# Accumulating DMAs for two block sums, and a third Strassen-Winograd step in one product

## The chip, the cores and the metric

The kernel runs on one core of a Trainium2 chip. A core has five engines with their own instruction queues: TensorE (PE in the profile) multiplies matrices into PSUM; VectorE (DVE), ScalarE (ACT) and GpSimd (POOL) work element by element; SyncE (SP) here only issues DMAs. ScalarE and GpSimd can issue DMAs too. An engine runs its queue in order and waits on semaphores for the others. The metric is the time of one execution on the device in microseconds, taken as the median of several runs.

## The reference

Two layers with residuals, on x of 8 sequences x 256 tokens x 1024 features, float32:

```python
# layer one: a dense layer plus a gated mixture of 8 rank-16 corrections
base   = einsum('btd,od->bto', x, W)
logits = einsum('btd,ed->bte', x, Wr) + 5.0 * one_hot(language_ids)[:, None, :]
topw, topi = top_k(logits, 2);  gates = the softmax of topw, put at topi
h      = einsum('btd,erd->bter', x, A)
x      = x + base + 2.0 * einsum('bter,bte,eor->bto', h, gates, B)
# layer two: each sequence has its own full 1024 x 1024 matrix of 16
x      = x + einsum('bsi,boi->bso', x, weight[adapter_ids])
```

The residual x is carried in the weights: the identity is added to W and to each adapter's matrix.

## The kernel before

**Layer one** is a product of a 1024 x 1024 matrix with 1024 x 2048 values, cut into 2 x 2 blocks: weights w11 to w22, inputs x11 to x22, results y11 to y22 (512 features by 1024 tokens each). The Strassen-Winograd scheme replaces the eight block products by seven, named "1" to "7" and run in the order 1, 5, 2, 6, 3, 7, 4. Their operands are sums of blocks, built in place by VectorE (`w_sum`, `x_sum`). Each block product is itself done by seven smaller products in the same way, in PSUM accumulators A, X and B. Function `product` writes one out by hand. Each smaller product is four matmuls in the source (two contraction chunks by two row tiles, 512 columns), which the profile counts as eight instructions, because it lists two per float32 matmul. The operands s1 to s3 and t1 to t3 are sums of quarters that `make_subs` plans for VectorE.

A y block has four quarters, `y[:, 0]` to `y[:, 3]`, each 128 partitions x 1024 elements (512 KB). A product adds its results to the quarters of `base` and writes them into those of `dest`. Where there is no base, `evict` is a copy on ScalarE; where there is one, it is an add on VectorE.

**The third step.** One of the seven smaller products multiplies two raw, unsummed quarters: X += a(0,1) b(1,0). With `deep` set, `third` does this one by seven still smaller products too, the pieces 1 to 7 (128 x 128 by 128 x 256, one contraction chunk). VectorE prepares six small operands ahead (r1, q1, r2, q2, r4, q4, planned no earlier than place 4 of the product before) and two more in between (`ops3`: r3, q3). Pieces 2, 3, 4 go into X. Pieces 1, 5, 6, 7 go into two single PSUM banks, and `take` adds them to the quarter `dest[:, 0]`. Products 5, 2 and 3 take this step; product 4 takes it twice; 6 and 7 (`make_subs(..., False)`) do not. Products 5, 2, 3 and 4 also accumulate low-rank matmuls (hg by b_sb or bdiff) into their accumulators; 6 and 7 have none.

The order inside a product with the third step is: A; piece 1; half of B; piece 5; A again, then VectorE's first add out of A (line 622, into quarter 1); piece 6; the other half of B and its add into quarter 3; pieces 2, 3, 4, 7 with their takes and the add of X into quarter 0; A a third time, then the second add out of A (line 644, into quarter 3); B and its add into quarter 1; A a last time (line 667) and its add into quarter 2.

**The filling work.** VectorE's other tasks stand in the list `todo` as (cost in us, earliest place, function). `pump(place)` is called at places 1 to 7 of every product. It takes the sum of all costs left, divides it by the places left (this one included), and issues tasks from the head of the list, leaving out those whose place has not come, until the rest of that share is 0.3 or less; at place 7 everything goes. Tasks are issued into the engine's queue where they stand, so this order is VectorE's order.

**The sums of whole y blocks.** `join(y12, y21)` and `join(y22, y21)` (lines 834 to 838) add y21 onto y12 and onto y22, a quarter per task, with the earliest places 4, 5, 6, 7 for quarters 0, 3, 1, 2. The first runs during product 3, which finishes y12 and leaves y21 alone; the second during product 7, which adds to y21. Product 7 and then product 4 rewrite y21. y12 and y22 hold the second half of the tokens, with which layer two starts.

**Layer two** runs per sequence (`adapt`), with one level of the same scheme. Its matrices are loaded by SyncE (`load_w1`, eight sets of four 1 MB blocks) into the room of x and w blocks of layer one that are no longer read; `prep_w1` and `prep_y` form the sums.

Of the kernel before, what the change touches and what calls it, by code (L numbers as in the profile page):

```python
# [12 lines left out]
ALU = mybir.AluOpType  # L13
# [12 lines left out]
def kernel(  # L26
# [26 lines left out]
    nc = tc.nc  # L53
# [56 lines left out]
    def yq(ij):  # L110

        return flat(yb[ij]).rearrange("p (q m n) -> p q m n", q=4, m=2)
# [103 lines left out]
    def tt(out_, x, y, op):  # L216
        nc.vector.tensor_tensor(out_, x, y, op)  # L217

    def add(out_, x, y):
        tt(out_, x, y, ALU.add)  # L220

    def minus(out_, x, y):
        tt(out_, x, y, ALU.subtract)
# [109 lines left out]
    todo = []  # L333
# [13 lines left out]
    def us(n):  # L347
        return (n + 151) / 960
# [9 lines left out]
    def x_sum(fn, out_, x, y):  # L358
        return pieces(fn, xb[out_], xb[x], xb[y], 4)
# [65 lines left out]
    def make_subs(key, w, x, further=True):  # L425

        def a(i, j):
            return wb[w][:, 2 * j : 2 * j + 2, i * OQ : (i + 1) * OQ]  # L430

        def b(i, j):
            return xb[x][:, 2 * i : 2 * i + 2, j * TQ : (j + 1) * TQ]

        t = {}

        def op(name, fn, x, y, first):
            pool = sub2 if name[1] == "2" else sub1
            width = OQ if name[0] == "s" else TQ

            def run():
                t[name] = pool.tile([P, 2, width], F32, name=f"{name}_{key}", tag=name)
                fn(t[name], *(t[v] if isinstance(v, str) else v for v in (x, y)))

            return us(2 * width), first, run

        def late_s():
            minus(t["s2"], a(0, 1), t["s2"])

        def late_t():  # L450
            minus(t["t2"], b(1, 0), t["t2"])

        deep = third(key, lambda: a(0, 1), lambda: b(1, 0)) if further else None
        subs[key] = (a, b, t, (late_s, late_t), deep)
        return [
            op("s1", add, a(1, 0), a(1, 1), 3),
            op("t1", minus, b(0, 1), b(0, 0), 3),
            op("s2", minus, "s1", a(0, 0), 3),
            op("t2", minus, b(1, 1), "t1", 3),
            op("s3", minus, a(0, 0), a(1, 0), 5),  # L460
            op("t3", minus, b(1, 1), b(0, 1), 5),
        ] + (deep[0] if further else [])
# [221 lines left out]
    def load_w1(u, *which):  # L684
        if u >= NB:
            return
        if u not in adapter:
            b = order[u]
            adapter[u] = nc.sync.value_load(aid_i[0:1, b : b + 1], min_val=0, max_val=NAD - 1)
        for ij in which:  # L690
            i, g = int(ij[0]) - 1, int(ij[1]) - 1
            nc.sync.dma_start(
                rawset[u % 2][ij], w1[bass.ds(adapter[u], 1), g, i].rearrange("a p k n -> p (a k) n")
            )
# [139 lines left out]
    y11, y12, y21, y22 = (yq(ij) for ij in IJ)  # L834

    def join(y, x):

        return [(1.22, p, lambda q=q: add(y[:, q], y[:, q], x[:, q])) for q, p in ((0, 4), (3, 5), (1, 6), (2, 7))]


    opening("1", y21)
# [45 lines left out]
    todo += t3[2:]  # L887
    product("6", y21, y21)
    load_w1(0, "21")
    todo += make_subs("7", "21", "11", False)  # L890
    t4 = x_sum(minus, "21", "21", "12")
    todo += t4[:2]
    todo += join(y12, y21)
    product("3", y22, y12, 2, 1)
    load_w1(0, "12", "22", "11")
    todo += t4[2:]
    todo += make_subs("4", "22", "21")
    todo += join(y22, y21)
    product("7", y21, y21)
    load_w1(1, "12", "11")  # L900
    todo += prep_w1(0, 0)
# [59 lines left out]
```

## Time and profile before

| | us |
|---|---|
| median of 3 runs | 427.61 (427.39 to 428.8) |
| profiled execution, its own time | 427.97 |
| its span, first to last instruction | 426.2 |
| TensorE busy | 421.2 (99%) |
| VectorE busy | 293.4 (69%) |
| ScalarE busy | 40.0 (9%) |
| GpSimd busy | 2.0 (0%) |
| product 3 on TensorE | from 145.6 to 176.1 |
| product 7 on TensorE | from 176.1 to 200.1 |
| product 4 on TensorE | from 200.1 to 230.2 |

The times of the products are read from TensorE's timeline. In those three stretches TensorE is busy throughout (30.5, 24.0 and 30.1 us), and VectorE for 23.6, 21.7 and 23.3 us. The DMA engines are busy 33%, 32% and 21% of them. A timeline line gives the start, the duration, the engine, the line of the kernel, the operation, what it writes and reads, the tile shapes and how many like instructions are merged; a bracket is idle time before it and what ended it. Line 217 is the helper that issues every VectorE sum, so such lines are told apart by their tiles: `y<-A,y` is an add out of accumulator A, `s` and `t` are operands of the next product, `r` and `q` those of the third step.

### The profile page before, as it was taken

What the parts mean: (1) busy time and instruction counts of PE and PEld (TensorE: products, weight loads), DVE (VectorE), ACT (ScalarE), POOL (GpSimd) and SP (SyncE); (2) the same over time, 40 slices, a digit from 0 to 9 for tenths busy, and PEclk for the clock granted to TensorE, in tenths of its full rate; (3) what the DMA queues carried; (4) which work ended last, traced back from release to release, by engine and by line L of the source; (5) the groups of instructions that cost most, each with busy time, mean ns of one, the idle gap of its engine ahead of it and who ended that gap; (6) DMA issues with size and microseconds to landing.
All of it is one profiled execution on the core that took longest, in us unless ns stands there. A gap on an engine that the chain in (4) does not pass through costs nothing.

```text
span 426.2 us, 3410 instructions
## 1 busy us (share of the span) xinstructions
PE 421.2 (99%) x1264; PEld 220.4 (52%) x1264; DVE 293.4 (69%) x409; ACT 40.0 (9%) x67; POOL 2.0 (0%) x10
## 2 busy tenths in 40 slices
PE   8999999999999999999999999999999999999996
PEld 6579975445444454444455444444444444444574
DVE  1646799857999859889598766665747666665531
ACT  2010122020000000000000101010110101010110
POOL 1000000000000000000000000000000000000000
PEclk9999999999999999999999999999999999999999
DMA  8995000000000230720202285565648385550202
GB/s 282 381 399 222 2 0 2 0 0 2 0 0 1 74 125 6 288 100 0 100 0 98 98 282 213 212 214 213 248 173 309 110 288 205 204 192 0 98 2 99
DMA packets 14305, 55.83 MB, mean 131 GB/s; under 512 B 1232, under 2 KB 3536, under 8 KB 9808
## 3 DMA queue, kind: packets, MB, share of 16 engines
q1 hardware_dynamic: 12976, 54.68, 35.7%
q10 hardware_dynamic: 1248, 0.93, 0.7%
q8 instruction: 10, 0.16, 0.2%
q14 instruction: 7, 0.06, 0.0%
q0 software_dynamic: 64, 0.00, 0.0%
HBM read 47.22 MB, written 8.39 MB: 130 GB/s over the span
## 4 chain that ended last, share of the span: by engine, by line
PE 95%; DVE 3%; issue 0%; POOL 0%; ACT 0%; POOLq 0%; DVEq 0%
PE A L741 23%; PE A L479 22%; PE B L741 13%; PE B L479 12%; PE ps_h L245 7%; PE X L741 6%; PE X L479 4%; PE A_last L799 3%; PE P L411 1%; DVE y L217 1%; DVE x L217 1%; PE X L411 1%; PE idle L495 1%; PE A L411 1%; DVE w L217 1%; PE P_1a L411 0%
## 5 line engine op out<-in xcount | busy, mean ns | idle before, releaser
L741 PE MATMUL B<-x,x 128*128 128x512 f32 x128 | 57.5, 592 | 0.0
L479 PE MATMUL A<-t,s 128*128 128x512 f32 x112 | 50.3, 592 | 0.0
L741 PEld LDWEIGHTS B<-x,x 128*128 128x128 f32 x128 | 24.3, 190 | 29.8 <-issue 29.7
L741 PE MATMUL A<-w,x 128*128 128x512 f32 x88 | 39.6, 592 | 0.0
L741 PE MATMUL A<-w,y 128*128 128x512 f32 x88 | 39.1, 592 | 0.0
L217 DVE TENSOR_TENSOR w<-w,w 128x1024 f32<-128x1024 f32 x24 | 28.9, 1221 | 14.0 <-PE A L741 14.0
L245 PEld LDWEIGHTS ps_h<-y,x 128*128 128x128 f32 x256 | 31.7, 190 | 3.3 <-issue 2.9
L479 PEld LDWEIGHTS A<-t,s 128*128 128x128 f32 x112 | 21.2, 190 | 22.9 <-issue 22.5
L245 PE MATMUL ps_h<-y,x 128*128 128x136 f32 x256 | 31.9, 279 | 0.0
L217 DVE TENSOR_TENSOR y<-A,y 128x1024 f32<-128x1024 f32 x19 | 23.2, 1221 | 11.5 <-PE A L479 11.3
L741 PEld LDWEIGHTS A<-w,x 128*128 128x128 f32 x88 | 16.7, 190 | 21.0 <-issue 21.0
L741 PEld LDWEIGHTS A<-w,y 128*128 128x128 f32 x88 | 16.7, 190 | 20.6 <-issue 20.6
L467 ACT COPY z<-A 128x512 f32<-128x512 f32 x21 | 12.3, 586 | 157.9 <-PE A L741 157.9
L479 PE MATMUL B<-t,s 128*128 128x512 f32 x56 | 25.9, 594 | 0.0
L479 PE MATMUL A<-x,w 128*128 128x512 f32 x56 | 25.3, 592 | 0.0
L479 PE MATMUL B<-x,s 128*128 128x512 f32 x48 | 21.6, 592 | 0.0
L217 DVE TENSOR_TENSOR x<-x,x 128x1024 f32<-128x1024 f32 (+1 forms) x20 | 19.3, 1002 | 0.0
L479 PE MATMUL A<-t,w 128*128 128x512 f32 x40 | 18.1, 595 | 0.1
L217 DVE TENSOR_TENSOR y<-B,y 128x1024 f32<-128x1024 f32 x12 | 14.6, 1219 | 5.1 <-PE B L479 5.1
L217 DVE TENSOR_TENSOR z<-X,z 128x512 f32<-128x512 f32 x8 | 5.5, 691 | 17.9 <-PE X L741 15.9
L217 DVE TENSOR_TENSOR t<-x 128x1024 f32<-128x1024 f32 x14 | 17.0, 1217 | 0.3 <-DMA x<-xT_dram 0.3
L217 DVE TENSOR_TENSOR t<-x,t 128x1024 f32<-128x1024 f32 x14 | 17.0, 1217 | 0.0
(166 smaller groups left out, 468.2 us busy)
## 6 DMA issues: line engine op xcount, KB each, us to landing
x<-w_dram SPq DMA_DIRECT2D x24, 1024.0 KB, 4.9
w<-w_dram SPq DMA_DIRECT2D x8, 1024.0 KB, 4.7
out_dram<-z SPq DMA_DIRECT2D x15, 512.0 KB, 3.0
x<-xT_dram SPq DMA_DIRECT2D x6, 1024.0 KB, 13.3
w<-wT_dram SPq DMA_DIRECT2D x3, 1024.0 KB, 15.5
x<-xT_dram SPq DMA_DIRECT2D x4, 256.0 KB, 3.9
x<-xT_dram SPq DMA_DIRECT2D x2, 512.0 KB, 6.8
w<-w11T_dram SPq DMA_DIRECT2D x1, 512.0 KB, 5.6
```

What stands on the lines that cost most here:

```text
L217: nc.vector.tensor_tensor(out_, x, y, op)
L245: nc.tensor.matmul(ps[v][:, u * EA : (u + 1) * EA], lhsT=xk(k, j, c)[:, ts(r, P)], rhs=aw_sb[:, k, :], start=(first and k == some[0] and u ...
L411: nc.tensor.matmul(out_, lhsT=l, rhs=r, start=(n in (1, 5)), stop=True, skip_group_check=True)
L467: nc.scalar.copy(dest, acc)
L479: nc.tensor.matmul(acc[:, m, :], lhsT=l, rhs=r, start=(first and i < len(ms)), stop=(i >= len(steps) - len(ms)), skip_group_check=True,)
L495: nc.tensor.matmul(idle[:, 0, :P], lhsT=ident, rhs=ident, start=True, stop=True)
L741: nc.tensor.matmul(accs[name], lhsT=lhs[:, k // 2, k % 2, :], rhs=rhs[:, k, :], start=(first and k == 0), stop=(k == KH - 1), skip_group_c ...
L799: nc.tensor.matmul(acc, lhsT=lhs[:, k // 2, k % 2, :], rhs=rhs[:, k, ts(v, m)], start=(first and k == 0), stop=(k == KH - 1), skip_group_c ...
```

## The change

The tasks of `join` become DMAs that GpSimd issues: each reads a quarter of y21 and adds it to the quarter of y12 or y22 where that lies, in SBUF. Their cost in `todo` becomes 0.0 and their places stay. They move ahead of the tasks of `make_subs` in the list. Product 7's `make_subs` no longer has `False`, so that product 7 takes the third step, and its six small operands r1 to q4 join the tasks that product 3 issues.

```diff
     def join(y, x):
 
-        return [(1.22, p, lambda q=q: add(y[:, q], y[:, q], x[:, q])) for q, p in ((0, 4), (3, 5), (1, 6), (2, 7))]
+        return [
+            (0.0, p, lambda q=q: nc.gpsimd.dma_start(y[:, q], x[:, q], accum_op=ALU.add))
+            for q, p in ((0, 4), (3, 5), (1, 6), (2, 7))
+        ]
...
     product("6", y21, y21)
     load_w1(0, "21")
-    todo += make_subs("7", "21", "11", False)
+    todo += join(y12, y21)
+    todo += make_subs("7", "21", "11")
     t4 = x_sum(minus, "21", "21", "12")
     todo += t4[:2]
-    todo += join(y12, y21)
     product("3", y22, y12, 2, 1)
     load_w1(0, "12", "22", "11")
     todo += t4[2:]
+    todo += join(y22, y21)
     todo += make_subs("4", "22", "21")
-    todo += join(y22, y21)
     product("7", y21, y21)
```

## The prediction

> **What bounds the kernel now.** I read the busy line, the chain, and then the timelines of TensorE and VectorE through layer one, the stage that the change touches.
>
> ```profile
> PE 421.2 (99%) x1264; PEld 220.4 (52%) x1264; DVE 293.4 (69%) x409; ACT 40.0 (9%) x67; POOL 2.0 (0%) x10
> PE 95%; DVE 3%; issue 0%; POOL 0%; ACT 0%; POOLq 0%; DVEq 0%
> ```
>
> TensorE is busy 99% of the span and its matmuls are 95% of the chain that ended last. Time is therefore gained only by removing TensorE work, and lost only by making TensorE wait. Product 7, in TensorE's timeline (start, duration, instruction):
>
> ```profile
> 176.06 3.60 PE L479 MATMUL A<-x,w 128*128 128x512 f32 x8
> 179.50 3.60 PE L479 MATMUL B<-t,s 128*128 128x512 f32 x8
> 182.93 3.60 PE L479 MATMUL A<-t,s 128*128 128x512 f32 x8
> 186.36 3.60 PE L479 MATMUL X<-x,w 128*128 128x512 f32 x8
> 189.80 3.60 PE L479 MATMUL A<-t,s 128*128 128x512 f32 x8
> 193.23 3.60 PE L479 MATMUL B<-x,s 128*128 128x512 f32 x8
> 196.66 3.60 PE L479 MATMUL A<-t,w 128*128 128x512 f32 x8
> ```
>
> Groups start every 3.433 us without a gap: four source-level matmuls are eight instructions of 0.429 us. A 128x256 piece (two instructions) paces at 0.43 us. Products 5, 2, 3 and 4 already take the third step. Product 2 shows what it can do (two lines of TensorE's timeline, one of VectorE's, one of the weight loads' waits in that stretch: total, times, longest):
>
> ```profile
> 114.33 1.88 PE L479 MATMUL B<-hg,bdiff 128*128 128x512 f32 x4
> 116.29 1.98 PE L479 MATMUL A<-t,w 128*128 128x512 f32 x4
> 115.02 1.22 DVE L217 TENSOR_TENSOR y<-A,y 128x1024 f32<-128x1024 f32 x1
> PEld A L479 <- DVE y L217: 0.9, 1, 0.9
> ```
>
> The last A group was due at 114.33 + 4 x 0.429 = 116.05. It started at 116.29, 0.05 after VectorE's add out of A ended (116.24). So this bank, read by VectorE between two uses, is the place where VectorE can hold TensorE. Product 3 runs the same order without x pieces in it (VectorE's timeline):
>
> ```profile
> 156.15 1.22 DVE L217 TENSOR_TENSOR y<-A,y 128x1024 f32<-128x1024 f32 x1 [2.88 <-PE A L479]
> 157.29 0.41 DVE L217 TENSOR_TENSOR y<-P,y 128x256 f32<-128x256 f32 x1
> 157.62 0.68 DVE L217 TENSOR_TENSOR s<-w,s 128x512 f32<-128x512 f32 x1
> 159.09 1.23 DVE L217 TENSOR_TENSOR y<-B,y 128x1024 f32<-128x1024 f32 x1 [0.78 <-PE B L479]
> 160.23 1.22 DVE L217 TENSOR_TENSOR t<-x,t 128x1024 f32<-128x1024 f32 x1
> 161.36 0.69 DVE L217 TENSOR_TENSOR s<-w 128x512 f32<-128x512 f32 x1
> 161.96 1.22 DVE L217 TENSOR_TENSOR t<-x 128x1024 f32<-128x1024 f32 x1
> 163.10 1.41 DVE L217 TENSOR_TENSOR y<-P,y 128x512 f32<-128x512 f32 x2
> 164.54 1.22 DVE L217 TENSOR_TENSOR y<-X,y 128x1024 f32<-128x1024 f32 x1
> 165.69 0.68 DVE L217 TENSOR_TENSOR s<-s,w 128x512 f32<-128x512 f32 x1
> 166.28 1.22 DVE L217 TENSOR_TENSOR t<-x,t 128x1024 f32<-128x1024 f32 x1
> 167.42 1.22 DVE L217 TENSOR_TENSOR y<-A,y 128x1024 f32<-128x1024 f32 x1
> ```
>
> From the first add out of A to the second: 11.27 us. With the bubble before B closed up (159.09 becomes 157.62 + 0.60 = 158.22, so 0.87 less) it is 10.40 us of back-to-back work. Product 3's low-rank matmuls give that stretch time. Product 7 has none.
>
> **What the skill says.** The Trainium skill's "DMA: Bandwidth & Descriptors", section "Anatomy of one DMA — SWDGE (gpsimd) path", prices a GpSimd DMA at about 2.0 us plus bytes / 436 GB/s: 3.2 us (estimate) for 512 KB. The trace's nearest rows agree in size: 512 KB stores land after 3.0 us, 1 MB loads after 4.7 to 4.9, GpSimd's two tiny DMAs after 4.4 to 4.6. "Collectives: The Full Stack", "The bandwidth ceiling", says an adding transfer reads two sources and costs double the reading, not the add: 1.2 us more (estimate); no row here shows an accumulating DMA. "SBUF — State Buffer", "Who interferes with whom", infers that a VectorE tensor_tensor does not block descriptor generation; untested here. "TensorE: Matmul & The Clock Gate", section on HAM oscillation, puts the idle gap that lowers the clock at about 3.4 us; the trace has no such gap after the opening.
>
> **The change, part by part.**
>
> 1. *Product 7's third step, TensorE.* Removed: the X group, four matmuls, 3.43 us. Added: seven pieces, 7 x 0.43 = 3.00. Gain 0.43 us, directly on the bound.
>
> 2. *Joins leave VectorE.* Eight adds at a pitch of 1.135 us, 9.1 us less of VectorE work. TensorE waits for none of them in products 3, 7, 4 (its only waits there are its own issue, 0.2 us each), so this alone is worth 0.
>
> 3. *Third step, VectorE.* In product 3, six small subtractions: 3 x 0.20 + 3 x 0.34 = 1.6 us, at places 6 and 7, in time the joins (4.5 us) leave. Free; without that room they would delay piece 5 of product 7, 5.5 us after product 3's end. In product 7: the 1.13 us X add stays, added are takes 1, 6 (0.34 each), 7, 5 (1.44 together) and r3, q3 (0.54): 2.7 us.
>
> 4. *Where pump puts work in product 7.* The list is now 2.44 (two x21 quarters) + 5.74 + 2.14 = 10.33 us, the joins count 0. Place 1: share 10.33/7 = 1.475; one quarter leaves 0.255, under 0.3, stop. Place 2: 9.11/6 = 1.518; the second quarter. Place 3: s1, t1. Place 4: join q0, s2, t2. So the second quarter falls into the stretch between the two reads of A.
>
> 5. *The stretch.* Product 7 starts at 176.06 as before. The A group that feeds the first add ends after A, p1, half B, p5, A = 2 x 3.433 + 0.43 + 1.717 + 0.43 = 9.44 us: 185.50. VectorE starts 0.27 later (as 156.15 against 155.88 in product 3): 185.77. It then has 10.40 + 1.13 (second quarter) = 11.53 us, every input of which is by then ready. The second add runs 197.30 to 198.52, and A can be written from 198.57. TensorE wants it after p6, half B, p2 to p4, p7, A, B: 185.50 + 0.43 + 1.72 + 1.29 + 0.43 + 3.43 + 3.43 = 196.23. Stall 2.34 us. This is unhidden: product 4 and layer two keep TensorE full to the end, so the delay is handed on. In product 4 VectorE is no later relative to TensorE (it drains at 204.1, before the first piece ends at 205.87).
>
> 6. *The DMAs and their waits.* POOL is otherwise empty after 2.7 us, so nothing queues behind these but one another; SP's loads keep their order. Each transfer must read y21 before the next product rewrites that quarter, a new wait on VectorE, behind which its whole queue stands. y12's issue at 165.8 (q0), 168.7, 172.7 (q1), 177.6; rewrites at 180.1, 189.0, 185.8, after 200. Least room: q1, 13.1 us. For y22: q0 issues at 195.6, is wanted at 205.9 (VectorE has 3 us of idling behind it); q1 10.5 us plus about 2 of slack. Low end of a transfer: 3.0. High: 4.5 + 2.4 (double data), doubled again for sharing with two 1 MB weight loads, 12. I take 5. Up to 12 all are hidden by the room; past 13 each us is a us. Four more DMA waits on VectorE: at most 0.05 each (the semaphore step seen above), 0.1 in the stretch; I take 0, since they are satisfied early. A gain from this part is excluded: nothing waited for the joins.
>
> 7. *Weight loads.* The load for x12's second half waits for the second x21 quarter, 7 us later than now (about 188.9 + pitch); landing near 194 to 200, it is first used past 240. Free.
>
> Sum: -0.43 + 2.34 = +1.91 us. The profiled execution took 427.97 (span 426.2, 1.8 around it), so 429.88; the median of the runs, 427.61, becomes 429.5.
>
> **Rivals.**
>
> *VectorE keeps up (ends not slower).* The stall vanishes or shrinks below the measurement if the second x21 quarter runs before the first add out of A, where VectorE idles 2.9 us. Place: pump's place 1. Price: 1.13 us; then stall 1.21, net +0.78, 428.4. It decides at a share of 0.3; the sum gives 0.255, so it needs an error of mine in the list. The same mechanism with the stretch 0.64 us shorter than I count also ends within measurement. Speaking for the bare gain (427.2): VectorE's total in product 7, about 20 us of 23.6, fits on average. Against: product 2's measured stall, with more TensorE time to spare.
>
> *Accumulating DMAs are slow.* If a transfer's data takes d, q0, q3 and q1 follow one another: 3 + 3d must fit 20 us before VectorE's first add in product 7, and about 18.4 in product 4 with its slack. It decides at d = 5.1 to 5.7 us. At d = 6: 1.0 + 2.6 on top, 433; at 8: about 445. For: the row is missing, and loads share the engines (share 0.41 to 0.51 from 165 to 190). Against: 1 MB lands in 4.9.
>
> *The clock drops.* A stall of 2.3 us is under the skill's 3.4; if it counted, a window at half speed adds some 1.7: 431.2.
>
> That the joins stay on VectorE can't be: the instruction is gone from its queue.
>
> **How the numbers follow.** Forecast 0.70, 429.0 to 430.3 (stall 1.8 to 3.1). VectorE keeps up 0.13: 0.12 within, 0.01 faster. Slow DMAs 0.14. Clock 0.03. A measurement of this kernel tells about 0.3% (1.28 us) from no change: bounds 426.33 and 428.89. Slower: 0.70 + 0.14 + 0.03 = 0.87. The range 428.4 to 433 leaves out the bare gain (0.07) and the worst DMA cases (0.09).
>
> **What would show it.** TensorE should show one gap of about 2.3 us before product 7's last A group, released by VectorE's add into y21, and no other new one; product 7 without it 23.6 us. VectorE should run without idling from 185.8 to 198.5, with an x21 piece after the s subtraction. The DMAs should land about 5 us after issue, with no VectorE wait on a DMA. The prediction fails if that gap is under 1.7 us, if a DMA wait appears ahead of an add into y21, or if product 4 stalls as well.

## The result, and the profile after

The change made the kernel slower: 430.82 us median of 4 runs (430.63 to 431.87) against 427.81 (the three runs of the kernel before and one more), a ratio of 1.0072 with a 95% interval of 1.0048 to 1.0096. Run again later, five runs gave 431.11 against 427.90, and 1.0072 (1.0059 to 1.0086). The prediction said 429.5, range 428.4 to 433.0.

The busy line and the chain (engines' shares of the work that ended last) of the kernel after:

```profile
PE 421.5 (98%) x1270; PEld 221.6 (52%) x1270; DVE 288.6 (67%) x413; ACT 40.1 (9%) x67; POOL 9.0 (2%) x18
PE 92%; DVE 6%; issue 0%; POOL 0%; ACT 0%; DVEq 0%; POOLq 0%
```

TensorE's share of the chain fell from 95% to 92% and VectorE's doubled, although VectorE does 4.8 us less in all (288.6 against 293.4). It is one place. TensorE's timeline at the end of product 7:

```profile
193.27 3.60 PE L479 MATMUL B<-x,s 128*128 128x512 f32 x8
199.02 3.70 PE L479 MATMUL A<-t,w 128*128 128x512 f32 x8 [2.15 <-DVE y L217]
202.56 3.60 PE L479 MATMUL A<-x,w 128*128 128x512 f32 x8
```

The last A group was due at 193.27 + 3.43 = 196.70 and started 2.32 us late, released by VectorE's add into y21. (The bracket, 2.15, counts from the modelled end of the matmul before, 3.60 after its start; both measures name the same gap.) Three lines of VectorE's timeline, the first add out of A, the x21 quarter, and the second add:

```profile
186.22 1.22 DVE L217 TENSOR_TENSOR y<-A,y 128x1024 f32<-128x1024 f32 x1 [2.86 <-PE A L479]
188.29 1.22 DVE L217 TENSOR_TENSOR x<-x,x 128x1024 f32<-128x1024 f32 x1
197.75 1.22 DVE L217 TENSOR_TENSOR y<-A,y 128x1024 f32<-128x1024 f32 x1
```

197.75 - 186.22 = 11.53 us; VectorE does not idle between them. TensorE has no other new gap.

To compare kernels apart from the opening, I read off TensorE's timeline when product 3 starts and how long it is from there to the first matmul of layer two. That stage holds all that was changed; from its end to the issue of the last output every one of the 13 profiles takes 192.94 or 192.95 us. The gap is counted from the due start, and each ratio is against runs of the kernel before taken beside it:

| kernel | product 3 starts | stage | gap before the last A | median, ratio (95%) |
|---|---|---|---|---|
| before | 145.58 | 84.59 | none | 427.81 to 427.96 |
| the change | 146.03 | 86.60 | 2.32 | 430.82, 1.0072 (1.0048, 1.0096) |
| joins only | 144.95 | 84.60 | none | 428.10, 1.0009 (1.0001, 1.0017) |
| step only | 146.35 | 86.58 | 2.29 | 430.85, 1.0067 (1.0054, 1.0080) |
| quarter first | 146.42 | 85.50 | 1.2 | 429.33, 1.0029 (1.0022, 1.0037) |
| late operands | 145.09 | 84.19 | none | 427.96, 1.0003 (0.9994, 1.0011) |
| late, joins on VectorE | 145.38 | 84.74 | none (0.46 in product 4) | 428.35, 1.0008 (0.9998, 1.0018) |
| twice the traffic | 146.59 | 94.72 | 1.0 (and 6.5 in the third step) | 438.66, 1.0246 (1.0231, 1.0262) |
| two more adds | 145.02 | 91.66 | 4.6 | 434.67, 1.0164 (1.0150, 1.0178) |

The stage grew by 2.01 us where the prediction had 1.91. The rest of the difference between these two profiled executions, 0.45 + 0.14 us, is a later start of product 3 and a longer end. But the medians of the runs grew by 3.0. The experiments were made to tell whether the gap is the third step's or the joins', and where the last us comes from.

### The profile page after: what moved, and what is told of

Read it like the earlier page. It is cut to its first block, busy times and chain, and to the rows that moved or that the text cites. A ratio compares the mean times of both kernels' runs of the same rounds, so it can differ in the third digit from the quotient of the medians.

```text
span 428.8 us, 3453 instructions
## 1 busy us (share of the span) xinstructions
PE 421.5 (98%) x1270; PEld 221.6 (52%) x1270; DVE 288.6 (67%) x413; ACT 40.1 (9%) x67; POOL 9.0 (2%) x18
## 3 DMA queue, kind: packets, MB, share of 16 engines
q1 hardware_dynamic: 12976, 54.68, 35.6%
## 4 chain that ended last, share of the span: by engine, by line
PE 92%; DVE 6%; issue 0%; POOL 0%; ACT 0%; DVEq 0%; POOLq 0%
PE A L741 22%; PE A L479 21%; PE B L741 13%; PE B L479 11%; PE ps_h L245 7%; PE X L741 6%; PE A_last L799 3%; PE X L479 3%; DVE y L217 3%; PE P L411 2%; DVE x L217 1%; DVE t L217 1%; PE X L411 1%; PE idle L495 1%; PE A L411 1%; DVE s L217 1%
## 5 line engine op out<-in xcount | busy, mean ns | idle before, releaser
L217 DVE TENSOR_TENSOR y<-A,y 128x1024 f32<-128x1024 f32 x19 | 23.2, 1220 | 16.3 <-PE A L479 13.3
L217 DVE TENSOR_TENSOR y<-P,y 128x512 f32<-128x512 f32 (+1 forms) x17 | 9.5, 561 | 11.1 <-PE P L411 10.4
```

## The experiments

**Each half alone.** First the accumulating joins without the third step (a diff against the kernel after):

```diff
-    todo += make_subs("7", "21", "11")
+    todo += make_subs("7", "21", "11", False)
```

> The joins as accumulating DMAs ahead of the operands, product 7 without the third step. If VectorE's stretch in product 7 is the whole cause: no gap on TensorE there, product 7 back at 24.0 us, time that of the kernel before (427.8, within 0.5). If the DMAs themselves cost (their traffic, their waits on VectorE, or the instructions that GpSimd gains), up to the 3.0 us of the change: a gap released by a DMA, or about 1 us spread over product 3, 7 or the opening, 428.8 to 430.8.

TensorE's timeline of the group that had the gap:

```profile
196.04 3.60 PE L479 MATMUL A<-t,w 128*128 128x512 f32 x8
```

The stage took 84.60 us, the same as before to 0.01; no gap, no wait on a DMA. The ratio of the runs is 1.0009, about 0.4 us, and their medians differ by 0.14. Some 0.2 us of it stands at the very end: from the issue of the last output to the end of the span it is 425.8 - 422.50 = 3.3 us, in every profile with GpSimd's transfers 3.2 to 3.3, without them 3.0 to 3.1.

Then the third step alone (a diff against the kernel before, whose joins stay as they are):

```diff
-    todo += make_subs("7", "21", "11", False)
+    todo += make_subs("7", "21", "11")
```

> The third step in product 7 alone; the joins stay VectorE adds where they stood. VectorE's stretch then loses the second x21 quarter (the fuller list puts both at place 1) and gains s2 (no change) and r1, q1, r2, q2 in place of it: 10.40 + 1.08 = 11.48 us, so a gap of about 2.3 us in the same place and 2.0 us more than before in product 7: 429.8. If the DMAs are what costs, no gap and about 427.4; if the DMAs were needed to make room for the step, clearly worse than the change, over 432.

TensorE's timeline in this kernel:

```profile
199.31 3.70 PE L479 MATMUL A<-t,w 128*128 128x512 f32 x8 [2.12 <-DVE y L217]
```

It is the same gap, 2.29 us, and the same stage (86.58). The stretch here runs from 186.54 to 198.04, 11.50 us: the x21 quarter is out of it, and r1, q1, r2, q2 are in. So the loss belongs to the third step, with product 4's operands where they stand. Moving the joins neither caused it nor prevented it, although it took 9 us of work off VectorE. The runs were 2.9 us slower, again more than the stage's 2.0.

**What stands in the stretch.** Two edits of the kernel after move VectorE's tasks out of it and take no work away:

```diff
-    todo += t4[2:]
+    todo += [(0.9, p, f) for us, p, f in t4[2:]]
```

> The change, with the planned cost of the last two x21 quarters set to 0.9 so that both fall at place 1, where VectorE idles. By the stretch theory it is 1.13 us shorter (10.40), the gap 1.2 us, the time 1.1 us under the change: 429.7. If DMAs or something outside product 7 set the loss, no difference: 430.8.

```diff
-    todo += make_subs("4", "22", "21")
+    todo += [(us, max(p, 5), f) for us, p, f in make_subs("4", "22", "21")]
```

> The change, with every operand of product 4 planned no earlier than place 5 of product 7. The stretch loses s1, t1, s2, t2 (3.47 us): 8.06 us, and VectorE's add out of A ends about 195.5 where TensorE wants A at 196.7 (times of the change's profile): no gap, product 7 takes 23.6 us, 2.4 us under the change and 0.4 under the kernel before: 428.4 against 430.8, or 427.4 against 427.8. If the DMAs cost about 1 us apart from the gap, it stays at 428.5 to 429.

With a planned cost of 0.9 both x21 quarters fall at place 1, into VectorE's idle time. VectorE's timeline there, and TensorE's at the gap:

```profile
181.31 2.35 DVE L217 TENSOR_TENSOR x<-x,x 128x1024 f32<-128x1024 f32 x2
198.30 3.70 PE L479 MATMUL A<-t,w 128*128 128x512 f32 x8 [1.05 <-DVE y L217]
```

The gap shrank by 1.1 us, the length of one quarter's subtraction, and the stage with it (86.60 to 85.50). With the operands of product 4 late, VectorE's second add out of A follows the add out of X directly, and TensorE runs through:

```profile
192.20 1.23 DVE L217 TENSOR_TENSOR y<-X,y 128x1024 f32<-128x1024 f32 x1
193.34 1.22 DVE L217 TENSOR_TENSOR y<-A,y 128x1024 f32<-128x1024 f32 x1
195.77 3.60 PE L479 MATMUL A<-t,w 128*128 128x512 f32 x8
```

VectorE finishes the second add at 194.56, 1.2 us before TensorE wants A. Product 7 takes 199.20 - 175.58 = 23.62 us and the stage 84.19, 0.40 less than in the kernel before: the whole 0.43 us of the saved piece, less rounding. The time of the runs does not show it (1.0003, 0.9994 to 1.0011). With the 0.2 us at the end set against it, about 0.2 would be left (an estimate), less than these runs can tell.

**Whether the joins have to be DMAs for that.** The late order with VectorE's joins, against the kernel before:

```diff
-    todo += make_subs("7", "21", "11", False)
+    todo += make_subs("7", "21", "11")
...
-    todo += make_subs("4", "22", "21")
+    todo += [(us, max(p, 5), f) for us, p, f in make_subs("4", "22", "21")]
```

> No accumulating DMAs: the joins as VectorE adds where the kernel before has them, product 7 with the third step, and product 4's operands not before place 5 of product 7. If moving the joins to DMAs is what makes room for the step, TensorE waits here in product 7 or at the start of 4 by 1 us or more. If only the order inside the stretch counts: product 7 in 23.6 us, at most a gap of 0.3 us before product 4's B, and a time within 0.3 us of the late-operand version with DMAs (428.0).

Product 7 takes 23.62 us here too. Product 4's first B then starts 0.46 us after it was due, held by VectorE (TensorE's timeline):

```profile
203.81 1.98 PE L479 MATMUL B<-t,s 128*128 128x512 f32 x4 [0.29 <-DVE y L217]
```

So the stage is 84.74. This is the only place found where the DMAs of the joins are worth something: 84.74 - 84.19 = 0.55 us, once the order is mended. The medians, 428.35 and 427.96, can't confirm so little: their ratios' intervals overlap.

**How much room the transfers had.** This kernel adds each quarter of y21 onto y11 as well while product 3 runs, so that the DMA engines carry twice as many joins there:

```diff
-            (0.0, p, lambda q=q: nc.gpsimd.dma_start(y[:, q], x[:, q], accum_op=ALU.add))
+            (0.0, p, lambda q=q, d=d: nc.gpsimd.dma_start(d[:, q], x[:, q], accum_op=ALU.add))
             for q, p in ((0, 4), (3, 5), (1, 6), (2, 7))
+            for d in ((y, y11) if y is y12 else (y,))
```

> The change, with every quarter of y21 that the first join adds onto y12 also added onto y11 by a second accumulating DMA (so the rows of the first half of the tokens come out wrong; only the traffic counts). In the change's profile the eight DMAs took 5.4% of 16 engines' span, 2.9 us of all engines each, and quarter 1's landed 10.9 us after its issue at 173.3, at 184.2, 2.0 us before VectorE rewrites it at 186.2. Three more DMAs ahead of it or beside it are 8.7 us: it lands near 193, VectorE's first add out of A starts then, and the delay is handed on in full: about 6.5 us over the change, 437.5. If the DMAs had ample room, as the prediction had it (up to 12 us hidden, 5 taken), the time stays at 430.8.

In the kernel after, the page has these lines on the queues (packets, MB, share of 16 engines; q0 carries the joins, q1 the loads and stores) and on the joins' issues (count, KB, median us to landing):

```profile
q1 hardware_dynamic: 12976, 54.68, 35.6%
q0 software_dynamic: 1216, 4.20, 5.4%
y<-y POOLq DMA_DIRECT2D x8, 512.0 KB, 6.6
```

In the span of 428.8 us, 5.4% is 23.2 us of all engines, 2.9 for each join. The loads and stores on q1 moved 54.68 MB in 35.6%, which is 1.46 us per 512 KB. So a join costs the DMA engines twice what a plain transfer of its size between SBUF and the chip's main memory does; no plain transfer from SBUF to SBUF was run. One by one, y12's quarters landed 4.8, 9.6, 10.9 and 10.8 us after issue, with 1 MB weight loads issued between them, and y22's after 4.5, 4.7, 5.1 and 8.1. The third of y12, quarter 1, was issued at 173.3 and landed at 184.2; VectorE rewrites that quarter of y21 at 186.2. With twice the traffic, VectorE's and TensorE's timelines:

```profile
194.90 1.23 DVE L217 TENSOR_TENSOR y<-A,y 128x1024 f32<-128x1024 f32 x1 [10.97 <-DMA y<-y]
196.51 1.22 PE L411 MATMUL P<-q,r 128*128 128x256 f32 x2 [6.37 <-DVE y L217]
```

VectorE waited for the DMA until 194.9, where it was due at 186.8, and handed the delay on. The expected landing (near 193) was right within 2 us, and the time came out 1.2 us above 437.5, with the granted clock at 0.50 from 196 to 200 us, after this gap. The transfers of the change were hidden, but by no more than 2.0 us.

**The last us.** Two things vary from run to run. The opening: product 3 began anywhere from 144.95 to 146.59 in these profiles, with the same instructions before it; the first group of four matmuls took from 1.98 to 3.62 us, where four take 1.88 later on. These are the two ends, from TensorE's timelines of joins only and of twice the traffic:

```profile
4.24 1.98 PE L479 MATMUL X<-x,w 128*128 128x512 f32 x4
4.24 3.62 PE L479 MATMUL X<-x,w 128*128 128x512 f32 x4
```

And the mean clock: of the nine timed runs of the change (four, and the five of the repetition below), six had 1.0 (430.09 to 431.11 us) and three 0.994 to 0.996 (431.35 to 431.87); none of 55 runs of the kernel before was under 0.998. (What they lack to 1.0 costs nothing: in the profile of the kernel before the granted clock is under 1.00 only from 420 us on, 0.94 on average, where TensorE has all but finished.) The step alone, with the same gap and no joins as DMAs, has two of its five runs at 0.994 and 0.996 too. So the change was run again, and the gap made longer with two more adds in the stretch.

> The change itself, for its time over more runs and a second profile. Product 3 to the first matmul of layer two took 86.60 us against 84.59, 2.0 more, but the runs 3.0 more. If the opening's start of the clock is what varies (product 3 began at 145.0 to 146.4 in six profiles), the median comes down to 430.0 to 430.4 and the stage is again 86.6. If a clock that drops after the gap adds to it in a part of the runs, the median stays near 430.8 and some runs show a mean clock of 0.996 or less and 1 us more.

```diff
+    todo += [(0.0, 2, lambda q=q: add(y11[:, q], y11[:, q], y11[:, q])) for q in (0, 1)]
     todo += t4[2:]
```

> The change with two more VectorE adds of 1024 elements in the stretch (y11 onto itself, so the first half of the tokens comes out wrong). By the stretch theory the gap grows by 2.27 us to 4.6 and the time by 2.3 us to 433.1. If a gap of this length lowers TensorE's clock, the matmuls after it run at half speed for some time: a mean clock of 0.995 or less and 1 to 2 us more, 434 to 435.

The change again had a stage of 86.61 us. The two adds made a gap of 4.6 us, as expected, but cost 5.06 us in the stage over the change, not 2.27. TensorE's timeline there, and the stage's busy times (us; busy us and instructions of TensorE, weight loads, VectorE, ScalarE, GpSimd; granted clock; DMA share; GB/s):

```profile
200.28 6.48 PE L479 MATMUL A<-t,w 128*128 128x512 f32 x8 [4.42 <-DVE y L217]
200.00:203.00 3.00, 2.72 (x3) 1.18 (x4) 3.00 (x4) 0.00 (x0) 0.86 (x1) 0.50 1.01 190
```

The clock read half just after the gap, and the group took 6.48 us instead of 3.70: 2.27 + 2.78 = 5.05 us. All five timed runs had a mean clock of 0.990 to 0.996. Three more profiles of the change were taken to find the same in it.

> The change once more, for its profile alone. In nine timed runs the span was 428.3 to 429.3 at a mean clock of 1.0 (six runs) and 429.6 to 430.1 at 0.994 to 0.996 (three). If the gap of 2.2 us lowers the clock in those runs in which the opening was early, a profile at 0.996 or less shows product 3 starting before 145.6 and the last A group of product 7 longer than 3.7 us by 1 to 3 us; a profile at 1.0 shows it starting at 145.9 or later and the group at 3.7. If the low clock comes from elsewhere, the two are not tied.

> As the first look: early opening with a low clock after the gap, or late opening with a full one.

> As the first look: early opening with a low clock after the gap, or late opening with a full one.

TensorE's last A group of product 7 and the granted clock after it (the third number from the end of a window's line), in the first of the three:

```profile
198.03 5.40 PE L479 MATMUL A<-t,w 128*128 128x512 f32 x8 [2.16 <-DVE y L217]
198.00:200.00 2.00, 1.97 (x4) 0.93 (x5) 2.00 (x3) 0.00 (x0) 0.86 (x1) 0.73 1.06 197
200.00:202.00 2.00, 2.00 (x4) 0.91 (x3) 1.58 (x4) 0.00 (x0) 0.86 (x1) 0.50 1.03 197
202.00:204.00 2.00, 2.00 (x5) 0.76 (x4) 0.53 (x1) 0.00 (x0) 0.00 (x1) 0.91 0.93 174
```

and in the second:

```profile
198.82 3.70 PE L479 MATMUL A<-t,w 128*128 128x512 f32 x8 [2.16 <-DVE y L217]
200.00:202.00 2.00, 2.00 (x6) 0.83 (x5) 2.00 (x4) 0.00 (x0) 0.07 (x1) 1.00 0.99 184
```

The same gap of 2.16 us (by the bracket), once with the clock at half after it and once without. Granted 0.73, 0.50 and 0.91 in three windows of 2 us make up for some 3.4 us at half (an estimate). It costs 5.40 - 3.70 = 1.70 us, and the stage is 88.30 us instead of 86.61. The third profile is like the first (5.40 us, 88.30). Product 3 began at 145.04 and 145.51 in the two with the half clock, and at 145.82, 146.03 and 146.38 in the three profiles of the change without.

So, in these five, the executions that gain time in the opening lose more of it after the gap. No run of the change gets both right: the fastest of its nine has a span of 428.3 us, where the kernel before reaches 425.4, which is 2.9 less and not 2.0. An estimate shows that this is enough for the last us. The start of product 3 in a run of the kernel before can be worked out from its span, less 84.59, 192.95 and 3.08 us for what follows. Give each of the 55 runs 2.01 us for the stage, 0.15 for the end, and 1.70 more if its product 3 began by 145.51: the median rises by 3.1 us, and 26 of the 55 have the half clock. The two measurements were 3.0 and 3.2 us, and five of twelve executions. With the line drawn just under 145.82, the earliest start seen with a full clock in a profile, it would be 3.5 us. The half clock lifts the early half of the runs above the late half, and the median falls among late runs with a full clock.

Why the opening and the clock after the gap go together stays open: no run here set the one to see the other, and the granted clock reads 1.00 through the opening, in slow ones (3.62 us for the first four matmuls) as in fast ones (1.98).

## Why the prediction was right, point by point

- *What bounds, and the place.* Right. TensorE was held at the one place named, the last A group of product 7.
- *Steps 1, 4 and 5, the third step and the stretch.* Right in mechanism and size: seven pieces save 0.43 us (23.62 us for product 7 where nothing holds it), the quarter fell at place 2 as worked out from the shares, the stretch was 11.53 us as predicted, the stall 2.32 against 2.34. The stage's sum was +2.01 against +1.91; the 0.10 is in the first A group after the gap, 3.70 us instead of 3.60 even at full clock.
- *Step 2, the joins leave VectorE.* Right that this alone is worth nothing: 84.60 against 84.59.
- *Step 3.* Right. No piece of product 7 waited for its small operands.
- *Step 6, the DMAs.* Right that they are hidden, wrong on the margin. The 5 us I took is what most of y22's transfers took (4.5 to 5.1). In product 3, with one another and the weight loads, they took up to 10.9, and 2.0 us were left of a room of 12.9 (13.1 in the sum). The bound of 12 held, but it does not come out of its terms: 4.5 + 2.4, doubled, is 13.8. "Collectives: The Full Stack" in the Trainium skill, "The bandwidth ceiling", has an adding transfer cost double the reading. This trace agrees in size, 2.9 us of the engines against 1.46, though it does not show the reads one by one. The end of the kernel, 0.2 us later with GpSimd's transfers, was not in the sum.
- *Step 7.* Right. No weight load arrived late.
- *The rivals.* "VectorE keeps up" did not occur; the quarter put first shows what it would have been: stage +0.91 where it had +0.78. "DMAs are slow" did not occur, but twice the traffic showed its price. "The clock drops" is where the point went wrong: I took it as a case apart, of 0.03, because a gap of 2.3 us is under the 3.4 us that "TensorE: Matmul & The Clock Gate" in the Trainium skill gives in its section on HAM oscillation. Here the measurement decides: after gaps of 2.16 us the clock fell, in two of the five profiles of the change and, by the mean clock, in five of its twelve executions, for 1.70 us each where it was profiled. The size (1.7) was right, and its chance of 0.03 was not.
- *The number.* The measured 430.82 lies in the range of 428.4 to 433.0, but above the 429.0 to 430.3 of the main case. The range reached it because it had been made wide for slow DMAs and a lower clock, and the chance given to the clock was small. That part was luck.

So what was missing from +1.91 was the clock after the gap, which comes with the early openings, and 0.2 us at the end of the kernel: together about 1 us of the 3.0 measured. That the clock falls after the gap is shown in profiles; that it makes up the rest of this 1 us in the medians is the estimate above.

## What to carry to other kernels

Where one engine is full, ask of a change not how much work it frees elsewhere but what it puts between two uses of the same accumulator: here 4.8 us less VectorE work went with a 2.0 us longer stage, and moving four operand sums behind one add took all of it back, and 0.4 us more that the time of the runs is too coarse to show. A filler that spreads work by an even share does not know such deadlines; a task's earliest place is the means to tell it. And price a gap on TensorE with the clock that may come after it, as well as with its length.

## What was not expected of the hardware

- TensorE's clock fell to half for about 3.4 us after a gap of 2.16 us in a part of the executions (two of five profiles). After a gap of 4.4 us it read 0.50 and 0.51 from 200 to 206 us, and after one of 6.4 us 0.50 from 196 to 200; every timed run of these two kernels had a mean clock of 0.990 to 0.996.
- An accumulating DMA from SBUF to SBUF, 128 partitions x 4 KB, took GpSimd 0.85 to 0.91 us to issue, landed after 4.5 us with the queues otherwise empty, and cost the DMA engines 2.9 us, twice a plain load or store of that size. VectorE's pace beside it was unchanged (1.13 us per 1024 elements).
